# Two graph layers with gathers: the first gathers ahead of the flag, own rows multiplied in their own round, finish in four parts

## The chip, the cores and the metric

The kernel runs on one core of a Trainium2 chip. The metric is the time of one execution on the device in microseconds (us); the median of the runs is given with their lowest and highest. One more execution was profiled: its trace has each instruction of each engine, and the lines shown come from it. The engines are TensorE (PE; its weight loads are PEld), VectorE (DVE), ScalarE (ACT), GpSimd (POOL) and SyncE (SP, which only issues DMAs here).

## The reference

6250 nodes with 512 features; 106,250 edges `src`, `dst`, sorted by `dst` (100,000 random ones, each in both directions, and a loop for each node). Two layers, each an average over neighbours, two products and a normalization:

```python
# layer 0 (edges gathered by src, averaged at dst)
x_l = x @ W_l.T + b_l
agg = segment_sum(x_l[src], dst); deg = segment_sum(1, dst)
x = layernorm(x + agg / max(deg, 1) + x @ W_r.T)
# layer 1 (edges gathered by dst, averaged at src)
msg = h[dst] @ W_neigh.T + b_neigh
neigh = segment_sum(msg, src) / max(deg, 1)
out = relu(h @ W_self.T + b_self + neigh)
y = h + out
x = layernorm(x + layernorm(y) * gamma + beta)
```

All in float32. Since a product is linear, the kernel averages the rows first and multiplies the average.

## The kernel before

**Sorting.** `Sorter` holds the edges of a layer as tiles of 128: `node` (whose average an edge belongs to) and `idx` (which row it brings), both [128, 896]. For layer 0 the order is given: `as_given` (L333) loads keys, values and the keys shifted by one, turns them with TensorE and counts neighbours that are out of order (`mixed`, L373). A branch on `mixed` (L895) would sort; it isn't taken with these inputs. `place` (L450) finds the windows of nodes, writes their starts `lo`, the offsets `rel`, and a `flag` (L492), 0 when the grouped form fits. Layer 1 is sorted on DVE and TensorE; its steps are handed to layer 0's rounds as `other` (`more`, L768).

**Pools.** A pool keeps, for each tile name, as many buffers as its `bufs` says; `const` has one. `idx` is named `f"idx{layer}"` (L228).

**Rounds.** `grouped` (L585) works in Q rounds (60 in layer 0, 66 in layer 1). Round g takes four windows of up to 32 nodes, one for each quarter of the edges; the last rounds have three. Its edges lie in three or four tiles per window, and each tile of a window is one gather: an indirect DMA on GpSimd that brings 128 rows of 512 floats (`fetch`, L613; `gather`, L608). The rows go into `rows`, ten buffers of four gathers each. `match` (L627) makes 0/1 matrices on DVE, `shrink` their column sums; `visits` (L691) adds the rows into `agg` with TensorE, a tile at a time; `count` and `average` make `mean`. `begin` (L675) loads the window's own rows with SP; for layer 0's rounds 56 and 57 with a gather on GpSimd (L683). `turn` transposes `own` or `mean` through the one PSUM buffer `tp`, copied out by ACT (L576); `dense` multiplies it with w_r or w_l into `po` (one buffer in layer 0, two in layer 1). `close` runs the first part of the finish, `store` the second, and writes the rows with SP, or in the last rounds with GpSimd.

**Order.** The order on each engine is the order in which the instructions are written: the loop at L778. In round g: the gathers of g + 1, visits(g) to the first two tiles, turn(g - 1, mean), dense(g - 1, own), store(g - 2), begin(g + 1), visits to the third tile, dense(g - 1, mean), turn(g, own), the rest of visits(g), count, average, close(g - 1), then a piece of layer 1's sort. Each engine has its own queue, and an instruction that waits holds up what is behind it in that queue. Layer 1's gathers read `h_d`, which layer 0 writes, so they begin when its last row is stored.

Of the kernel before, what the change touches and what calls it, by code (L numbers as in the profile page):

```python
# [19 lines left out]
C = 4  # L20
# [78 lines left out]
def kernel(  # L99
# [109 lines left out]
    class Sorter:  # L209
# [123 lines left out]
        def as_given(self):  # L333


            full = M - 1
            ints, f32 = [], []
            for i, (v, fill, skip) in enumerate(((self.key, NONE, 0), (self.val, 0, 0),
                                                 (self.key, NONE, 1))):
                t = self.pool.tile([P, blocks, P], I32, name=("key_i", "val_i", "next_i")[i])  # L340
                nc.vector.memset(t[:, full // P:, :], fill)
                eng = nc.sync
# [12 lines left out]
                if i < 2:  # L355
                    f = self.pool.tile([P, blocks, P], F32, name="srt", bufs=2)
                    nc.vector.tensor_copy(f, t)
                    f32.append(f)
            for f, o in zip(f32, (self.node, self.idx)):
                p = self.ps.tile([P, 2 * D], F32, name="turn")  # L360
# [3 lines left out]
                nc.vector.tensor_copy(o[:, D:W], p[:, D:W])  # L364
            nxt = ints[2]
            nc.vector.tensor_tensor(nxt, ints[0], nxt, op=ALU.is_gt)
            worst = self.pool.tile([P, 1], F32, name="worst")
# [3 lines left out]
            nc.tensor.matmul(p[:1, :1], worst, ones[:, :1], start=True, stop=True)  # L371
            self.mixed = const.tile([1, 1], I32, name=f"mixed{self.layer}")
            nc.vector.tensor_copy(self.mixed, p[:1, :1])  # L373

# [75 lines left out]
        def place(self):  # L450
# [6 lines left out]
            nc.vector.memset(bad, 0.0)  # L457
            if self.loops:
                nc.vector.tensor_copy(bad[:, 2 * NW + C:], self.odd)
            ends = self.ps.tile([P, 2 * D], F32, name="turn")  # L460
# [67 lines left out]


    def finish0(nr, po, own, some, work):  # L530
        po = po[:nr]
        nc.vector.scalar_tensor_tensor(po, biases["bl"][:nr], some[:nr], po,
                                       op0=ALU.mult, op1=ALU.add)
        v = work.tile([P, D], F32, name="v", bufs=1)
        both(v[:nr], po, own[:nr], ALU.add)
        mv, root = spread(v[:nr], nr, work)
# [5 lines left out]
    def finish1(nr, po, own, some, work):  # L542
        po = po[:nr]
        if some is None:
            both(po, po, biases["bs + bn"][:nr], ALU.add)
        else:
            nc.vector.scalar_tensor_tensor(po, biases["bn"][:nr], some[:nr], po,
                                           op0=ALU.mult, op1=ALU.add)
            both(po, po, biases["bs"][:nr], ALU.add)
        nc.vector.scalar_tensor_tensor(po, po, 0.0, own[:nr], op0=ALU.max, op1=ALU.add)  # L550
        mv, root = spread(po, nr, work)
# [32 lines left out]

    def grouped(s, table, w_n, w_s, layer, finish, dest, other):  # L585


        with tc.tile_pool(name=f"g{layer}", bufs=2) as work, tc.tile_pool(
            name=f"gp{layer}", bufs=1, space=PSUM
        ) as ps:  # L590
            M, NW, Q = s.M, s.NW, s.Q
            chunks, hots, state = {}, {}, {}
            ends = Q - 1, (NW - 1) % Q, (NW - 2) % Q
# [13 lines left out]

            def gather(t, m):  # L608
                nc.gpsimd.indirect_dma_start(  # L609
                    out=t, out_offset=None, in_=table,  # L610
                    in_offset=bass.IndirectOffsetOnAxis(ap=s.idx[:, m:m + 1], axis=0))

            def fetch(g):  # L613
                for t in ([-1] if g == 0 else []) + list(own_tiles(g)):
                    rows = work.tile([P, C, D], F32, name="rows", bufs=CHUNKS)
                    chunks[t] = {}
                    for c in windows(g):
                        m = c * (Q // 2 * s.pair) + t
                        if 0 <= m < M:
                            gather(rows[:, c, :], m)  # L620
                            chunks[t][c] = rows[:, c, :]

# [120 lines left out]

            def close(g):
                st = state[g]
                st["finish"] = finish(st["nr"], st["po"], st["own"], st["some"], work)
                next(st["finish"])

# [26 lines left out]
            shrink(0)  # L775
            fetch(0)
            begin(0)
            for g in range(Q + 1):  # L778
# [116 lines left out]
    with tc.If(mixed > 0):  # L895
# [20 lines left out]

    f0 = nc.values_load(s0.flag[:1, :1], min_val=0, max_val=2 * s0.NW + C)
    with tc.If(f0 == 0) as cmp:
        grouped(s0, x, *w0, 0, finish0, h_d, sort_and_place(s1))
    with cmp.Else():  # L920
        drain(sort_and_place(s1))
        plain(s0, x, *w0, 0, finish0, h_d)

# [4 lines left out]
    with tc.If(f1 == 0) as cmp:  # L928
        grouped(s1, h_d, *w1, 1, finish1, out, iter(()))
    with cmp.Else():  # L930
# [29 lines left out]
```

## Time and profile before

| | us |
|---|---|
| median of 3 runs | 2129.82 (2129.74 to 2130.59) |
| the profiled execution | 2130.99 |
| its span, first to last instruction | 2129.2 |
| first gather of layer 0 | 30.38 |
| first gather of layer 1 | 1111.16 |
| last gather | 2095.39 |

The granted TensorE clock was 0.984 of full speed on average. A page line of a group gives: line, engine, operation, output<-inputs, number | busy us, mean ns of one | idle us just before them and what ended it. A line of the timeline gives: start, length, engine, line, operation, output<-inputs, shape, number [idle before <- what ended it]. A line of the chain gives: start, length, what the end of the run depended on then. `issue` is time without a wait that the profile shows.

### The profile page before, as it was taken

The page shows a single profiled execution, that of the slowest core. Times are in us where ns is not written, and L with a number is a line of the kernel's source. Part 1 is how long each engine was busy: PE and PEld are TensorE (multiplying, and loading weights), DVE is VectorE, ACT ScalarE, POOL GpSimd, SP SyncE. Part 2 cuts the span into 40 slices and gives each one's busy share as a digit, 9 for nine tenths or more (in the row PEclk, how much of TensorE's full clock was granted, in tenths as well). Part 3 has the DMA queues.
Part 4 walks back from the last instruction along what each step waited for, and adds up shares of the span by engine and source line. Part 5 has one row for each costly group of instructions (what it writes and reads, how often), then busy time and mean ns, then how long its engine had stood idle before and what let it go on. Part 6 is the DMA issues. An engine that isn't in the chain of part 4 may idle for free.

```text
span 2129.2 us, 26081 instructions
## 1 busy us (share of the span) xinstructions
PE 1945.1 (91%) x7723; PEld 671.4 (32%) x7723; DVE 1185.0 (56%) x2495; ACT 314.6 (15%) x661; POOL 1554.9 (73%) x1638
## 2 busy tenths in 40 slices
PE   4699999999999998999879999999999999999996
PEld 1132333332323333433222333333333333333332
DVE  2574455564555564342433666666666666666576
ACT  0011111111111111111111111111111111111111
POOL 3777777777777777777747777777777777777773
PEclk9899999999999999999989999999999999999998
DMA  7787877878887878888757888888888888888883
GB/s 225 224 242 235 238 237 237 240 238 240 238 239 237 239 236 240 246 237 242 223 151 227 243 246 246 245 246 244 246 242 249 240 249 241 247 242 246 241 247 109
DMA packets 184527, 499.36 MB, mean 235 GB/s; under 512 B 43946, under 2 KB 46436, under 8 KB 184366
## 3 DMA queue, kind: packets, MB, share of 16 engines
q0 software_dynamic: 130128, 426.11, 67.8%
q1 hardware_dynamic: 51406, 65.89, 9.7%
q10 hardware_dynamic: 2832, 5.51, 0.7%
q8 instruction: 66, 1.08, 0.2%
q14 instruction: 95, 0.78, 0.1%
HBM read 464.74 MB, written 32.96 MB: 234 GB/s over the span
## 4 chain that ended last, share of the span: by engine, by line
DMA 32%; POOL 28%; PE 22%; issue 14%; DVE 3%; POOLq 0%; ACT 0%; SPq 0%; DVEq 0%; ACTq 0%
POOL rows L609 28%; DMA rows<-h_d,idx 17%; DMA rows<-in_x_dram,idx 14%; PE po L582 10%; PE agg L700 9%; PE tp L574 2%; DMA val_i<-in_dst_dram 0%; DVE stats L514 0%; PE turn L465 0%; DVE po L173 0%; DMA own<-in_x_dram,slots 0%; PE deg L709 0%; PE turn L438 0%; PE turn L294 0%; DVE agg L727 0%
## 5 line engine op out<-in xcount | busy, mean ns | idle before, releaser
L700 PE MATMUL agg<-rows,hot 128*32 128x512 f32 x4220 | 900.3, 612 | 134.0 <-DMA rows<-in_x_dram,idx 46.1
L609 POOL DMA_INDIRECT rows<-in_x_dram,idx x834 | 800.7, 960 | 266.4 <-issue 224.7
L609 POOL DMA_INDIRECT rows<-h_d,idx x785 | 744.9, 949 | 242.6 <-issue 200.3
L582 PE MATMUL po<-wa,meanT 128*128 128x512 f32 (+1 forms) x1008 | 466.0, 605 | 0.0
L582 PE MATMUL po<-wb,ownT 128*128 128x512 f32 (+1 forms) x1008 | 456.3, 596 | 0.1
L700 PEld LDWEIGHTS agg<-rows,hot 128*32 128x32 f32 x4220 | 157.0, 109 | 655.0 <-DMA rows<-in_x_dram,idx 242.0
L565 DVE TENSOR_SCALAR inv<-deg 128x1 f32<-128x1 f32 (+1 forms) x60 | 9.5, 158 | 490.4 <-PE deg L709 490.4
L582 PEld LDWEIGHTS po<-wa,meanT 128*128 128x128 f32 (+1 forms) x1008 | 180.2, 188 | 286.7 <-issue 256.5
L582 PEld LDWEIGHTS po<-wb,ownT 128*128 128x128 f32 (+1 forms) x1008 | 181.8, 190 | 183.6 <-issue 183.4
L576 ACT COPY ownT<-tp 128x512 f32<-128x512 f32 (+1 forms) x126 | 73.3, 582 | 800.6 <-PE tp L574 800.6
L718 DVE TENSOR_SCALAR loops<-deg 128x1 f32<-128x1 f32 (+1 forms) x66 | 10.4, 158 | 310.9 <-PE deg L709 302.4
L173 DVE SCALAR_TENSOR_TENSOR srt<-srt 128x448 f32<-128x448 f32 (+3 forms) x313 | 180.4, 617 | 4.0
L731 ACT ACTIVATE mean<-agg,inv 128x512 f32<-128x512 f32 (+1 forms) x126 | 86.6, 687 | 359.3 <-DVE some L568 147.2
L640 DVE TENSOR_REDUCE hotb<-hot 128x128 bf16<-128x512 f32 (+1 forms) x126 | 133.8, 1062 | 0.1
L518 ACT ACTIVATE rstd<-mv,eps 128x1 f32<-128x1 f32 (+1 forms) x192 | 56.5, 294 | 438.9 <-DVE mv L516 435.6
L576 ACT COPY meanT<-tp 128x512 f32<-128x512 f32 (+1 forms) x126 | 73.1, 580 | 193.0 <-PE tp L574 192.9
L173 DVE SCALAR_TENSOR_TENSOR hot<-rel,cols 128x640 f32<-128x640 f32 x126 | 98.1, 778 | 0.2 <-DVE bs L173 0.2
L574 PEld LDWEIGHTS tp<-ident,mean 128*128 128x128 f32 (+1 forms) x504 | 52.8, 141 | 110.7 <-issue 43.5
L574 PE MATMUL tp<-ident,mean 128*128 128x128 f32 (+1 forms) x504 | 82.8, 287 | 4.8 <-ACT mean L731 4.8
L574 PEld LDWEIGHTS tp<-ident,own 128*128 128x128 f32 (+1 forms) x504 | 62.7, 141 | 72.8 <-issue 69.7
L574 PE MATMUL tp<-ident,own 128*128 128x128 f32 (+1 forms) x504 | 75.7, 273 | 5.4 <-DMA own<-in_x_dram,slots 5.4
L524 DVE TENSOR_SCALAR po<-po,mv,rstd 128x512 f32<-128x512 f32 (+1 forms) x66 | 54.0, 818 | 2.4
(151 smaller groups left out, 900.1 us busy)
## 6 DMA issues: line engine op xcount, KB each, us to landing
own<-h_d SPq DMA_DIRECT2D x261, 64.0 KB
out_dram<-y SPq DMA_DIRECT2D x250, 64.0 KB
own<-in_x_dram SPq DMA_DIRECT2D x230, 64.0 KB
h_d<-y SPq DMA_DIRECT2D x227, 64.0 KB
rows<-in_x_dram,idx POOLq DMA_INDIRECT x834
rows<-h_d,idx POOLq DMA_INDIRECT x785
wa<-in_L_gnn_W_l_dram ACTq DMA_DIRECT2D x1, 1024.0 KB
wb<-in_L_gnn_W_r_dram ACTq DMA_DIRECT2D x1, 1024.0 KB
```

Source lines behind the costliest of these rows:

```text
L173: nc.vector.scalar_tensor_tensor(o, a, 1.0, b, op0=ALU.mult, op1=op)
L518: nc.scalar.activation(root[:nr], mv[:nr, 1:2], AF.Sqrt, bias=eps[:nr])
L524: nc.vector.tensor_scalar(y, v, mv[:nr, 0:1], root[:nr], op0=ALU.subtract, op1=ALU.mult)
L565: nc.vector.tensor_scalar(inv[:nr], deg, 1.0, None, op0=ALU.max)
L574: nc.tensor.transpose(p[:, k, :nr], v[:nr, k * P:(k + 1) * P], ident[:nr, :nr])
L576: nc.scalar.copy(t[:, :, :nr], p[:, :, :nr])
L582: nc.tensor.matmul(po[:nr], aT[:, k, :nr], w[:, k, :], start=first and k == 0, stop=end and k == NK - 1)
L609: nc.gpsimd.indirect_dma_start(out=t, out_offset=None, in_=table, in_offset=bass.IndirectOffsetOnAxis(ap=s.idx[:, m:m + 1], axis=0))
L640: nc.vector.tensor_reduce(hb[:, 0, :], hots[g][:, s.X * C:n * C].rearrange("p (v c) h -> p (c h) v", c=C), axis=mybir.AxisListType.X, op=A ...
L700: nc.tensor.matmul(agg[H * c:H * (c + 1), :], hot[:, C * (s.X + v) + c, :], chunks[t][c], start=t == ts[0], stop=t == ts[-1])
L718: nc.vector.tensor_scalar(st["loops"][:nr], deg[:nr, 1:2], 1.0, None, op0=ALU.add)
L731: nc.scalar.mul(st["mean"][:nr], st["agg"][:nr], st["inv"][:nr])
```

## The change

Layer 0's first gathers (19, for tiles -1 to 3) are issued ahead of everything that depends on keys: their indices come by four small loads on ACT's queue straight from the list of values (`first_rows`), into a tile of `const` named `idx0`. The `mixed` branch is gone; its number goes into the flag, and the sort stands in the flag's other branch. In `as_given` the shifted keys are loaded by ACT, keys are turned first, and the values' turn comes back as a function that runs after `place`. The `rows` buffers lie in a pool of their own that both layers use. In the loop dense(g, own) is now in round g, after average(g); in the last round it stands ahead of the last visits. turn(g, own) stands ahead of dense(g - 1, mean). The finish runs in four parts: `ready`, two `follow`, `store`. finish0 adds bias and own rows before the product; finish1 adds own rows and beta at the start and then needs two operations for normalizing, gamma, beta and own rows.

```diff
@@ as_given
-            for i, (v, fill, skip) in enumerate(((self.key, NONE, 0), (self.val, 0, 0),
-                                                 (self.key, NONE, 1))):
+            for i, (v, fill, skip, eng) in enumerate((
+                (self.key, NONE, 0, nc.sync), (self.key, NONE, 1, nc.scalar),
+                (self.val, 0, 0, nc.sync),
+            )):
...
+            def columns(t, o):
+                f = self.pool.tile([P, blocks, P], F32, name="srt", bufs=2)
+                nc.vector.tensor_copy(f, t)
                 p = self.ps.tile([P, 2 * D], F32, name="turn")
                 for b in range(blocks):
                     nc.tensor.transpose(p[:, b * P:(b + 1) * P], f[:, b, :], ident)
                 nc.scalar.copy(o[:, :D], p[:, :D])
                 nc.vector.tensor_copy(o[:, D:W], p[:, D:W])
+            columns(key, self.node)
...
-            self.mixed = const.tile([1, 1], I32, name=f"mixed{self.layer}")
-            nc.vector.tensor_copy(self.mixed, p[:1, :1])
+            odd = self.pool.tile([1, 2], F32, name="mixed")
...
+            return lambda: columns(val, self.idx)
+
+        def first_rows(self):
+            n = 1 + self.half
+            self.idx0 = const.tile([P, C, n], I32, name="idx0")
+            for c in range(C):
+                a = c * (self.Q // 2 * self.pair) - 1
+                k = max(0, -a)
+                v = self.val[(a + k) * P:(a + n) * P]
+                nc.scalar.dma_start(self.idx0[:, c, k:], v.rearrange("(t p) -> p t", p=P))
@@ place
-            if self.loops:
-                nc.vector.tensor_copy(bad[:, 2 * NW + C:], self.odd)
+            nc.vector.tensor_copy(bad[:, 2 * NW + C:], self.odd)
@@ finish0
-        po = po[:nr]
-        nc.vector.scalar_tensor_tensor(po, biases["bl"][:nr], some[:nr], po,
+        v = work.tile([P, D], F32, name="v")
+        nc.vector.scalar_tensor_tensor(v[:nr], biases["bl"][:nr], some[:nr], own[:nr],
                                        op0=ALU.mult, op1=ALU.add)
-        v = work.tile([P, D], F32, name="v", bufs=1)
-        both(v[:nr], po, own[:nr], ALU.add)
+        yield
+        both(v[:nr], po[:nr], v[:nr], ALU.add)
+        yield
@@ finish1
+        add = work.tile([P, D], F32, name="add")
+        both(add[:nr], own[:nr], biases["be"][:nr], ALU.add)
+        yield
...
-        normalize(po, po, mv, root, nr)
-        both(po, po, biases["ga"][:nr], ALU.mult)
-        both(po, po, biases["be"][:nr], ALU.add)
+        nc.vector.reciprocal(root[:nr], root[:nr])
+        nc.vector.scalar_tensor_tensor(po, po, mv[:nr, 0:1], biases["ga"][:nr],
+                                       op0=ALU.subtract, op1=ALU.mult)
         y = work.tile([P, D], F32, name="y")
-        both(y[:nr], po, own[:nr], ALU.add)
+        nc.vector.scalar_tensor_tensor(y[:nr], po, root[:nr], add[:nr],
+                                       op0=ALU.mult, op1=ALU.add)
@@ the loop of rounds
             if g < Q:
                 visits(g, slice(0, 2))
-            if g:
-                turn(g - 1, "mean")
-                dense(g - 1, "own")
             if g > 1:
                 store(g - 2)
             if g + 1 < Q:
                 begin(g + 1)
+            end = g == Q - 1
+            if g:
+                turn(g - 1, "mean")
+            if g < Q and not end:
+                visits(g, slice(2, 3))
             if g < Q:
-                visits(g, slice(2, 3))
+                turn(g, "own")
             if g:
                 dense(g - 1, "mean")
+                follow(g - 1)
+            if end:
+                visits(g, slice(2, 3))
+                dense(g, "own")
             if g < Q:
-                turn(g, "own")
                 visits(g, slice(3, None))
                 count(g)
                 average(g)
             if g:
-                close(g - 1)
+                follow(g - 1)
+            if g < Q:
+                if not end:
+                    dense(g, "own")
+                ready(g)
@@ the order of the whole
+    rpool = ctx.enter_context(tc.tile_pool(name="rows", bufs=1))
...
-    s0.as_given()
+    s0.first_rows()
+    first = {t: gathered(s0, x, t, range(C), s0.idx0) for t in range(-1, s0.half)}
+    rest = s0.as_given()
     biases["bl"] = row_bcast(b_l, "bl_t")
     w0 = load_weights(w_l, w_r, 0)
-    mixed = nc.values_load(s0.mixed[:1, :1], min_val=0, max_val=P)
-    with tc.If(mixed > 0):
-        make_signs(spool)
-        drain(s0.runs())
     s0.place()
+    rest()
```

`gathered` issues one tile's gathers for the given windows, as `fetch` did, into `rows` of the new pool; with `idx0` it takes the indices from the small tile.

More of the change, by code (lines that the diff above doesn't have):

```diff
@@ L336, in as_given @@
             full = M - 1
-            ints, f32 = [], []
-            for i, (v, fill, skip) in enumerate(((self.key, NONE, 0), (self.val, 0, 0),
-                                                 (self.key, NONE, 1))):
-                t = self.pool.tile([P, blocks, P], I32, name=("key_i", "val_i", "next_i")[i])
+            ints = []
+            for i, (v, fill, skip, eng) in enumerate((
+                (self.key, NONE, 0, nc.sync), (self.key, NONE, 1, nc.scalar),
+                (self.val, 0, 0, nc.sync),
+            )):
+                t = self.pool.tile([P, blocks, P], I32, name=("key_i", "next_i", "val_i")[i])
                 nc.vector.memset(t[:, full // P:, :], fill)
-                eng = nc.sync
                 a = full // P
@@ L354, in as_given @@
                 ints.append(t)
[L355 to L359, printed above, removed]
+            key, nxt, val = ints
+            def columns(t, o):
+                f = self.pool.tile([P, blocks, P], F32, name="srt", bufs=2)
+                nc.vector.tensor_copy(f, t)
                 p = self.ps.tile([P, 2 * D], F32, name="turn")
@@ L364, in as_given @@
                 nc.vector.tensor_copy(o[:, D:W], p[:, D:W])
-            nxt = ints[2]
-            nc.vector.tensor_tensor(nxt, ints[0], nxt, op=ALU.is_gt)
+            columns(key, self.node)
+            nc.vector.tensor_tensor(nxt, key, nxt, op=ALU.is_gt)
             worst = self.pool.tile([P, 1], F32, name="worst")
@@ L371, in as_given @@
             nc.tensor.matmul(p[:1, :1], worst, ones[:, :1], start=True, stop=True)
-            self.mixed = const.tile([1, 1], I32, name=f"mixed{self.layer}")
-            nc.vector.tensor_copy(self.mixed, p[:1, :1])
+            odd = self.pool.tile([1, 2], F32, name="mixed")
+            nc.vector.memset(odd, 0.0)
+            nc.vector.tensor_copy(odd[:, :1], p[:1, :1])
+            self.odd = odd
+            return lambda: columns(val, self.idx)
[7 more added lines that the diff above has]
+                nc.scalar.dma_start(self.idx0[:, c, k:], v.rearrange("(t p) -> p t", p=P))
         def unpack(self):
@@ L550, in finish1 @@
         nc.vector.scalar_tensor_tensor(po, po, 0.0, own[:nr], op0=ALU.max, op1=ALU.add)
+        yield
         mv, root = spread(po, nr, work)
         yield
-        normalize(po, po, mv, root, nr)
-        both(po, po, biases["ga"][:nr], ALU.mult)
-        both(po, po, biases["be"][:nr], ALU.add)
+        nc.vector.reciprocal(root[:nr], root[:nr])
+        nc.vector.scalar_tensor_tensor(po, po, mv[:nr, 0:1], biases["ga"][:nr],
+                                       op0=ALU.subtract, op1=ALU.mult)
         y = work.tile([P, D], F32, name="y")
-        both(y[:nr], po, own[:nr], ALU.add)
+        nc.vector.scalar_tensor_tensor(y[:nr], po, root[:nr], add[:nr],
+                                       op0=ALU.mult, op1=ALU.add)
         mv, root = spread(y[:nr], nr, work)
@@ L583, in project, with gathered, grouped @@
                              start=first and k == 0, stop=end and k == NK - 1)
-    def grouped(s, table, w_n, w_s, layer, finish, dest, other):
+    def gathered(s, table, t, windows, idx):
+        rows = rpool.tile([P, C, D], F32, name="rows", bufs=CHUNKS)
+        got = {}
+        for c in windows:
+            m = c * (s.Q // 2 * s.pair) + t
+            if 0 <= m < s.M:
+                at = idx[:, m:m + 1] if idx is s.idx else idx[:, c, t + 1:t + 2]
+                nc.gpsimd.indirect_dma_start(
+                    out=rows[:, c, :], out_offset=None, in_=table,
+                    in_offset=bass.IndirectOffsetOnAxis(ap=at, axis=0))
+                got[c] = rows[:, c, :]
+        return got
+    def grouped(s, table, w_n, w_s, layer, finish, dest, other, chunks):
         with tc.tile_pool(name=f"g{layer}", bufs=2) as work, tc.tile_pool(
@@ L591, in grouped @@
             M, NW, Q = s.M, s.NW, s.Q
-            chunks, hots, state = {}, {}, {}
+            hots, state = {}, {}
             ends = Q - 1, (NW - 1) % Q, (NW - 2) % Q
@@ L606, in own_tiles @@
                              g // 2 * s.pair + (s.pair if g % 2 else s.half))
[L608 to L611, printed above, removed]
             def fetch(g):
                 for t in ([-1] if g == 0 else []) + list(own_tiles(g)):
[L615 to L621, printed above, removed]
+                    chunks[t] = gathered(s, table, t, windows(g), s.idx)
             def visit_tiles(g):
@@ L742, in dense, with ready, follow @@
                         v == "own", v == "mean")
-            def close(g):
+            def ready(g):
                 st = state[g]
                 st["finish"] = finish(st["nr"], st["po"], st["own"], st["some"], work)
+                next(st["finish"])
+            def follow(g):
+                st = state[g]
                 next(st["finish"])
@@ L775, in grouped @@
             shrink(0)
-            fetch(0)
+            if not chunks:
+                fetch(0)
             begin(0)
@@ L914, in sort_and_place @@
         yield True, s.place
-    f0 = nc.values_load(s0.flag[:1, :1], min_val=0, max_val=2 * s0.NW + C)
+    f0 = nc.values_load(s0.flag[:1, :1], min_val=0, max_val=2 * s0.NW + C + 2)
     with tc.If(f0 == 0) as cmp:
-        grouped(s0, x, *w0, 0, finish0, h_d, sort_and_place(s1))
+        grouped(s0, x, *w0, 0, finish0, h_d, sort_and_place(s1), first)
     with cmp.Else():
         drain(sort_and_place(s1))
+        drain(s0.runs())
         plain(s0, x, *w0, 0, finish0, h_d)
@@ L928 @@
     with tc.If(f1 == 0) as cmp:
-        grouped(s1, h_d, *w1, 1, finish1, out, iter(()))
+        grouped(s1, h_d, *w1, 1, finish1, out, iter(()), {})
     with cmp.Else():
```

## The prediction

> **What bounds it now.** I read the page first (engines, groups), then GpSimd's rows in order of time, then both layers' ends in the timeline and the chain. The page:
>
> ```profile
> span 2129.2 us, 26081 instructions
> PE 1945.1 (91%) x7723; PEld 671.4 (32%) x7723; DVE 1185.0 (56%) x2495; ACT 314.6 (15%) x661; POOL 1554.9 (73%) x1638
> ...
> L609 POOL DMA_INDIRECT rows<-in_x_dram,idx x834 | 800.7, 960 | 266.4 <-issue 224.7
> L609 POOL DMA_INDIRECT rows<-h_d,idx x785 | 744.9, 949 | 242.6 <-issue 200.3
> ```
>
> TensorE looks fuller (91%), but its busy time is stretched where it waits for rows; GpSimd is the pacemaker. One gather is 0.95 us plus 0.30 of issue: its rows start every 1.252 us for a thousand microseconds. 834 + 2 own gathers in layer 0 make 1047 us, 785 in layer 1 make 983. The rest of the span: 30 before the first gather, 24 between the layers' gathers (1087.6 to 1111.2), 33 after the last (2096.3), 12 lost between gathers. The timeline of the start and of layer 0's end, and the chain's pieces (start, length) there:
>
> ```profile
> 16.44 0.15 DVE L373 CAST mixed<-turn 1x1 int32<-1x1 f32 x1 [0.37 <-PE turn L371]
> 23.08 0.06 DVE L455 MEMSET node<- 128x1 f32 x1 [6.50 <-DVEq L895]
> 28.84 0.14 DVE L492 CAST flag<-nbad 1x1 int32<-1x1 f32 x1
> 30.38 1.13 POOL L609 DMA_INDIRECT rows<-in_x_dram,idx  x1 [12.70 <-issue]
> 54.36 0.95 POOL L609 DMA_INDIRECT rows<-in_x_dram,idx  x1 [0.30 <-issue]
> ...
> 1046.67 3.60 DMA own<-in_x_dram,slots
> 1050.41 1.09 PE tp L574 x4
> 1079.18 3.57 DMA rows<-in_x_dram,idx
> 1095.69 7.12 PE po L582 x16
> 1106.62 0.93 POOL L753 DMA_INDIRECT h_d<-y,slots  x1 [13.82 <-DVE y L524]
> 1111.16 1.00 POOL L609 DMA_INDIRECT rows<-h_d,idx  x1 [3.61 <-DVE hot L173]
> ```
>
> A gather cannot start before the flag; the mixed branch alone holds DVE 6.5 us. 54.36 is the 20th gather, the first of round 1. At the end the owner is TensorE: it stands still until 1050.3 for the own rows of round 56, then works through with one wait for rows (about 1.2 us, to 1082.75).
>
> **Part 1, the first gathers moved ahead of the flag.** When does the 20th gather start?
>
> - First index load, S. ACT issues four small loads from 0.76; one issue is about 0.45 (key_i's took 0.48). The first gather has no window 0, so it waits for the second: issued by 1.7, and a small load here lands some 1.95 after its issue began (last key piece 4.21, its cast 6.16). Each load is 512 or 640 pieces of 4 bytes. The Trainium skill, "DMA: Bandwidth & Descriptors", Rules for kernel authors, speaks against them: a last dimension that isn't contiguous becomes one descriptor per element. The nearest row is the 128-byte stores of the tail in the DMA view of 30 to 34 us:
>
> ```profile
> q1 hardware_dynamic: 901, 0.12, 18.3%
> ```
>
> 18.3% of 16 engines in 4 us over 901 packets is 13 ns each, so 40 per engine cost 0.5 us a load, not the price of a bulk load. S = 4.3; ends 3.3 (nothing shared with key_i) and 7.0 (60 ns each, two loads in a row).
> - Nineteen gathers: 53.10 - 30.38 = 22.7 to the start of the 19th.
> - They now lie beside DVE's casts. The Trainium skill, "SBUF — State Buffer", Who interferes with whom: a DVE operation in a two-port mode and GpSimd exclude each other for the whole instruction. The trace has it, two gathers beside one sign flip:
>
> ```profile
> 136.87 1.18 POOL L609 DMA_INDIRECT rows<-in_x_dram,idx  x1 [0.30 <-PE agg L700]
> 137.26 0.39 DVE L331 TENSOR_SCALAR srt<-srt 128x448 f32<-128x448 f32 x1
> 138.36 1.31 POOL L609 DMA_INDIRECT rows<-in_x_dram,idx  x1 [0.30 <-issue]
> ```
>
> They lose 0.23 + 0.36 to an operation of 0.39. By the rule two casts of 0.63 (L357) cost 1.3, scaled from the row 1.9; not all of a cast meets a gather: 1.0, ends 0 and 1.9.
> - A new wait. The small index tile has the same name as layer 0's index tile ("idx0"), in a pool with one buffer per name: the built program gives both one address, and both copies into the large one (ACT, then DVE) wait for all nineteen gathers to have landed; the next gather waits for ACT's. A gather lands 3.6 after its start (1046.67 to 1050.27); beside other loads up to 5.3 (31.81 to 37.06). I take 3.7: w_l and w_r, issued near 10, should be through by 25. Then ACT's copy 0.59 and two handshakes, 0.85.
>
> Sum: 4.3 + 22.7 + 1.0 + 3.7 + 0.85 = 32.6 against 54.4: **-21.8** (ends 30.4 and 37.8: -24.0, -16.6). What hides behind it: the key columns, comparison and placing follow as before, without the branch, so the flag comes near 20, the val transposes near 25, and GpSimd's flag read and branch (1.4, from 28.98 to 30.38) fit beside the landing. If key landed 7 us later, that cover is gone and every further microsecond counts. Behind ACT's waiting copy are six issues for layer 1's weights and biases (needed 1000 us later) and ACT's branch; ownT is wanted near 38. Behind DVE's copy are tail, branch and hot(0): TensorE starts near 34.5 instead of 34.1 and SP's tail store and own loads near 33, as before, but with all rows of round 0 there. Its slack takes this up: ten row tiles are 50 us of gathers. The 3 MB of layer 1's loads now run beside gathers, which stretches landings but no pace, since eight may be under way (10 us).
>
> **Part 2, own product in its own round.** Per round nothing is added: eight passes of 3.53, moved. While gathers set the pace it is free; a round needs 12.2 to 12.4 of TensorE (count to count, 2079.58, 2091.78, 2104.19) against 15.03 of twelve gathers. New waits inside: turn(own) for ACT's meanT copy (0.59, behind one tile of 1.0), dense(own) for DVE's read of po in layer 0 (0.69, behind the last tiles). DVE now waits in mid-round for dense(mean); behind it are count and the sort steps, due 12 us later, and DVE has 9 us of work there.
>
> At layer 0's end it costs. Own rows of rounds 56 and 57 come by gathers queued behind their round's rows. Today TensorE has finished dense(55, mean) when it stands; afterwards turn(56, own) is ahead of it, so at 1050.4 these 3.5 us are still to do. Both orders then have the same products left. Added: 3.5, 0.8 for turn(59, own) behind a copy with nothing between, 0.7 for the last meanT copy, no longer under dense(own). Taken off: the 1.2 wait for rows at 1082.75, 0.75 for the bias operation (L532, now early), 0.3 as the cold clock after the standstill costs some 2.3 on today's visits (1051.4 to 1055.0 for what takes 2.0) and would cost 2.0 on the product. **+2.7** (ends 0, if it catches up, and +5.5, if the cold clock of 1050 to 1054 lasts over the product). The jump to layer 1 is unchanged; its first gather waits on five fewer events of 0.05: -0.2.
>
> **Part 3, layer 1's end**, in timeline rows:
>
> ```profile
> 2104.19 0.25 PE L709 MATMUL deg<-ones_b,hotb 128*96 128x1 bf16 x2
> 2106.55 0.90 PE L574 MATMUL tp<-ident,mean 96*128 96x96 f32 x4 [2.12 <-ACT mean L731]
> 2107.25 4.97 PE L582 MATMUL po<-wb,ownT 128*96 128x512 f32 x8
> 2112.05 3.60 PE L582 MATMUL po<-wa,meanT 128*96 128x512 f32 x8
> 2115.68 0.69 DVE L173 SCALAR_TENSOR_TENSOR po<-po,bs 96x512 f32<-96x512 f32 x1 [2.11 <-PE po L582]
> ```
>
> No wait for rows is left here: TensorE is behind since round 62, so the last own product only moves ahead of the count: 2104.2 becomes 2107.7, turn(mean) begins 2.4 later as now, takes 0.5, meanT's copy, now bare, 0.6, and dense(mean), between the warm 3.60 and the cold 4.97, 4.3. It ends at 2115.5, today at 2115.6: -0.1. The finish gets shorter: 0.81 + 3 x 0.69 (normalize, gamma, beta, own) become two of 0.7, with gaps 7.95 becomes 6.4: **-1.5** (ends -3 and +1). The fewer DVE operations elsewhere lie under gathers: nothing.
>
> **Sum**: -21.8 + 2.7 - 0.2 - 1.6 = -20.9. The profiled execution took 2130.99 (span 2129.2, 1.8 around it), 1.2 above the median 2129.82; I apply the difference to the median: 2108.9.
>
> **Rivals.**
> A. As above, 2108.9 (its own range 2104 to 2115). Chance 0.70.
> B. The index loads are slow (100 ns a piece: two loads 8 us, S near 11) and everything after follows: 15 gained at the start, 2116. For: no row has 4-byte pieces. Against: the 13 ns. 0.11.
> C. The own product fills standstill at both ends after all (the chain gives TensorE 22% of the span): 3.5 off each end, instead of +2.7 and -0.1: 2099. For: dense(own) is in today's last chain at both ends. Against: only one wait for rows in the last 50 us. 0.12.
> D. **Slower**: TensorE becomes the bound in layer 1's rounds. Place: turn(mean), ACT's copy, turn(own), dense(mean) now run in series on one transpose buffer. The round would have to grow from 12.4 beyond 15.03; each 0.1 above costs 66 x 0.1 = 6.6, and the gain is gone at 15.35. Two bare copies with handshakes add 1.6 (14.0); at 15.6 the time is 2109 + 38 = 2147. 0.06. Nothing in the rows gives the missing 1.3.
> The first gathers not coming earlier at all can't be: no flag stands ahead of them. 0.01 for what I don't see.
>
> **Numbers.** The range reaches over B and C: 2101 to 2117. About 0.2% (4 us) is what a measurement here tells from no change. Faster 0.93 (A, B, C), same 0.01, slower 0.06.
>
> **What would show it.** First gather at 3.3 to 7; a hole of 3 to 5 us in GpSimd's rows before the 20th, ended by ACT's idx copy, the 20th near 32.6; then 1.252 without holes; TensorE standing until own of round 56 lands, longer than today's 5.4; layer 0's last h_d store about 19 after the shift, not 22; the finish after the last product about 6.4. Wrong: a first gather past 8, holes in GpSimd's rows in mid-layer (D), or layer 0's tail shorter than now (C).

## The result, and the profile after

| | us |
|---|---|
| before, median | 2129.81 (2129.74 to 2130.59) |
| after, median | 2165.5 (2162.78 to 2172.06) |
| ratio | 1.0169, 95% interval 1.0156 to 1.0182 |
| predicted | 2108.9 (2101 to 2117), faster |

The change makes the kernel 1.7% slower; the forecast had the wrong sign. (In two groups of runs below, e5 to e8 and e9 to e12, TensorE was granted 0.86 to 0.89 of its clock in the mean and the kernel before takes 2530 and 2534 us; their ratios stand against that, and "less clock" below means these runs.)

The page of the changed kernel, its span, engines, and the two groups of gathers:

```profile
span 2161.0 us, 26124 instructions
PE 1977.0 (91%) x7723; PEld 659.9 (31%) x7723; DVE 1127.5 (52%) x2431; ACT 310.2 (14%) x661; POOL 1574.0 (73%) x1638
...
L614 POOL DMA_INDIRECT rows<-in_x_dram,idx x834 | 808.3, 969 | 290.7 <-issue 206.8
L614 POOL DMA_INDIRECT rows<-h_d,idx x785 | 756.3, 963 | 241.7 <-issue 199.3
```

A gather takes 969 and 963 ns in the mean, where it took 960 and 949. The timeline of the start:

```profile
5.71 1.13 POOL L614 DMA_INDIRECT rows<-in_x_dram,idx  x1 [4.00 <-DMA idx<-in_src_dram]
33.07 0.59 ACT L364 CAST idx<-turn 128x512 int32<-128x512 f32 x1 [22.02 <-DMA rows<-in_x_dram,idx]
33.92 0.96 POOL L614 DMA_INDIRECT rows<-in_x_dram,idx  x1 [3.90 <-ACT idx L364]
34.31 0.66 SPq L940 DMA_DIRECT2D h_d<-tail  x1
36.67 23.58 SPq L713 DMA_DIRECT2D own<-in_x_dram  x8
60.12 1.09 PE L595 MATMUL tp<-ident,own 128*128 128x128 f32 x4 [19.25 <-DMA own<-in_x_dram]
70.97 1.00 POOL L614 DMA_INDIRECT rows<-in_x_dram,idx  x1 [12.12 <-PE agg L725]
81.20 1.09 DVE L258 TENSOR_TENSOR next_i<-key_i,val_i 128x896 int32<-128x896 int32 x1 [6.40 <-DMA val_i<-in_dst_dram]
91.16 6.12 PE L603 MATMUL po<-wb,ownT 128*128 128x512 f32 x8 [13.86 <-DVE inv L586]
98.57 1.39 POOL L614 DMA_INDIRECT rows<-in_x_dram,idx  x1 [17.88 <-PE agg L725]
```

The 20th gather is at 33.9, 20 us sooner than before. Then GpSimd stands twice (a "hole" below is such a stand between two gathers), 12.1 and 17.9 us, with all ten row tiles full, because TensorE stands: first for the own rows of round 0, then for VectorE, which is in the sort's first loads. Counted out in GpSimd's rows, for both kernels and for those experiments that ran where before takes 2130 (start of the named gather or store in us, ratio of times with its 95% interval; e14 also has a shorter finish for the last block):

| | 20th gather | 60th | last of layer 0 | first of layer 1 | last | last store | ratio |
|---|---|---|---|---|---|---|---|
| before | 54.4 | 106.4 | 1086.7 | 1111.2 | 2095.4 | 2123.9 | |
| after | 33.9 | 114.5 | 1102.8 | 1129.0 | 2124.5 | 2155.7 | 1.0169 |
| e1 weights early | 36.3 | 100.7 | 1086.8 | 1114.3 | 2118.0 | 2149.1 | 1.0121 (1.0104 to 1.0137) |
| e2 own name | 30.1 | 106.5 | 1092.3 | 1120.0 | 2121.7 | 2152.0 | 1.0153 (1.0136 to 1.0170) |
| e3 parts 2 and 3 | 54.7 | 107.1 | 1092.8 | 1120.5 | 2119.3 | 2151.1 | 1.0118 (1.0101 to 1.0135) |
| e4 part 1 | 34.5 | 106.6 | 1086.5 | 1110.3 | 2093.6 | 2120.0 | 0.9994 (0.9986 to 1.0003) |
| e13 part 2 | 54.8 | 107.3 | 1087.5 | 1116.2 | 2099.4 | 2139.9 | 1.0080 (1.0064 to 1.0097) |
| e14 part 1 mended | 30.4 | 80.7 | 1067.2 | 1091.0 | 2075.8 | 2102.1 | 0.9914 (0.9898 to 0.9931) |
| e15 parts 1, 2 mended | 30.5 | 80.6 | 1074.5 | 1102.8 | 2086.8 | 2123.1 | 0.9997 (0.9990 to 1.0003) |
| e16 the same, store behind | 30.4 | 80.4 | 1073.4 | 1101.8 | 2085.8 | 2113.5 | 0.9965 (0.9957 to 0.9972) |

The differences between the first two rows, column by column, account for the 31.8 between the two profiled spans (the medians differ by 35.7; the profiled execution of after is its fastest): -20.4 to the 20th gather, +28.5 to the 60th (the two holes), +8.0 to layer 0's last, +1.7 to layer 1's first, +11.3 to the last, +2.6 to the last store.

### The profile page after: what moved, and what is told of

Its sections match the earlier page's. It is cut to its first block, busy times and chain, and to the rows that moved or that the text cites. A ratio compares the mean times of both kernels' runs of the same rounds, so it can differ in the third digit from the quotient of the medians.

```text
span 2161.0 us, 26124 instructions
## 1 busy us (share of the span) xinstructions
PE 1977.0 (91%) x7723; PEld 659.9 (31%) x7723; DVE 1127.5 (52%) x2431; ACT 310.2 (14%) x661; POOL 1574.0 (73%) x1638
## 4 chain that ended last, share of the span: by engine, by line
PE 30%; DMA 27%; POOL 25%; issue 12%; DVE 3%; SPq 0%; ACT 0%; POOLq 0%; DVEq 0%; ACTq 0%
POOL rows L614 25%; PE po L603 15%; DMA rows<-in_x_dram,idx 14%; PE agg L725 11%; DMA rows<-h_d,idx 11%; PE tp L595 2%; DMA h_d<-tail 1%; DVE stats L528 0%; PE deg L734 0%; DVE hotb L665 0%; DMA own<-h_d 0%; DMA val_i<-in_dst_dram 0%; PE turn L294 0%; SPq L789 0%; DVE y L577 0%
## 5 line engine op out<-in xcount | busy, mean ns | idle before, releaser
L725 PE MATMUL agg<-rows,hot 128*32 128x512 f32 x4220 | 921.2, 606 | 98.3 <-DMA rows<-in_x_dram,idx 51.7
L614 POOL DMA_INDIRECT rows<-h_d,idx x785 | 756.3, 963 | 241.7 <-issue 199.3
L603 PE MATMUL po<-wb,ownT 128*128 128x512 f32 (+1 forms) x1008 | 466.3, 605 | 14.2 <-DVE inv L586 14.2
L603 PE MATMUL po<-wa,meanT 128*128 128x512 f32 (+1 forms) x1008 | 458.4, 598 | 3.8 <-ACT meanT L597 3.8
L173 DVE SCALAR_TENSOR_TENSOR po<-po,bs 128x512 f32<-128x512 f32 (+1 forms) x66 | 46.1, 699 | 346.4 <-PE po L603 346.4
L173 DVE SCALAR_TENSOR_TENSOR v<-po,v 128x512 f32<-128x512 f32 (+1 forms) x60 | 41.3, 689 | 254.2 <-PE po L603 254.2
L595 PE MATMUL tp<-ident,own 128*128 128x128 f32 (+1 forms) x504 | 82.9, 288 | 32.6 <-DMA own<-in_x_dram 19.3
L595 PEld LDWEIGHTS tp<-ident,own 128*128 128x128 f32 (+1 forms) x504 | 53.1, 142 | 138.1 <-issue 123.8
```

What stands on the lines that cost most here:

```text
L173: nc.vector.scalar_tensor_tensor(o, a, 1.0, b, op0=ALU.mult, op1=op)
L595: nc.tensor.transpose(p[:, k, :nr], v[:nr, k * P:(k + 1) * P], ident[:nr, :nr])
L603: nc.tensor.matmul(po[:nr], aT[:, k, :nr], w[:, k, :], start=first and k == 0, stop=end and k == NK - 1)
L614: nc.gpsimd.indirect_dma_start(out=rows[:, c, :], out_offset=None, in_=table, in_offset=bass.IndirectOffsetOnAxis(ap=at, axis=0))
L725: nc.tensor.matmul(agg[H * c:H * (c + 1), :], hot[:, C * (s.X + v) + c, :], chunks[t][c], start=t == ts[0], stop=t == ts[-1])
```

## The experiments

Four theories were tried. **T1**: the tail store (zeros into the last rows of `h_d`, 2048 pieces) lies beside 3 MB of layer 1's weights and holds the own loads, hence the first hole. **T2**: the second hole is VectorE's stand in the sort's loads, with GpSimd too far ahead. **T4**: operations of the new finish hold gathers back. **T5**: at layer 1's end a square root stands ahead of meanT's copy on ScalarE. (The expectations also name T3, that own rows are late for another reason than the tail; e1 ruled it out.)

**The first hole.** The DMA queues of the changed kernel from 40 to 48 us (q1 is SP's, q10 ScalarE's: packets, MB, share of 16 engines), then those of before around its tail store, 32 to 36 us:

```profile
q0 software_dynamic: 578, 1.90, 59.7%
q10 hardware_dynamic: 622, 1.16, 38.9%
q1 hardware_dynamic: 622, 0.08, 6.3%
```

```profile
q0 software_dynamic: 147, 0.51, 47.6%
q1 hardware_dynamic: 2064, 0.26, 44.9%
```

Before, the tail passed at 2064 packets in 4 us. Now its 128-byte packets take turns with the weights' packets of some 1.9 KB: 622 against 622, and in the order of their starts the two counts never differ by more than 3. From 50 to 54 us, with 34 packets left on ScalarE's queue, SP's passes 1053. The Trainium skill, "DMA: Bandwidth & Descriptors", Queues, rings and completion order, has each DMA engine take turns between the queues by packets; that fits. It calls 9 to 17 descriptors a typical packet; the records of the tail hold one piece of 128 bytes each, and they alternate singly. The chain of the changed kernel (start, length, what the end depended on), and the longest wait of SP's queue among the own loads:

```profile
34.31 21.57 DMA h_d<-tail
...
56.70 3.17 DMA own<-in_x_dram
59.87 0.25 issue
60.12 1.09 PE tp L595 x4
...
SPq L713 <- DMA h_d<-tail: 5.6, 1, 5.6
```

SP's issue of the first own load took 12.3 (36.67 to 48.97), and the third, at 55.89, was issued only when the tail had landed.

e1, the weights' loads alone moved:

```diff
+    w1 = load_weights(w_neigh, w_self, 1)   # and the four row_bcasts: moved up, from behind the tail
     s0.place()
     rest()
```

> The changed kernel with one edit: layer 1's weight and bias loads are issued ahead of the placing and the val columns, not behind ScalarE's late copy into idx. Theory T1 (the tail store takes turns with 3 MB of weights and holds the own loads, and the second hole only follows from the lead lost in the first): the tail store is through in about 5 us instead of 21.6, own rows of round 0 land near 41 instead of 60, no hole over 2 us in GpSimd's rows between 34 and 110, the 60th gather near 86 instead of 114.5; time 2137 (2133 to 2143), still above the kernel before, since the gathers' longer cadence and the ends stay. Rival T2 (the second hole has a cause of its own, VectorE's wait for the sort's loads with a lead that ten row tiles can't carry): the first hole of 11.8 goes, one of 10 or more near 80 stays; 2148 to 2154. Rival T3 (own rows are late for another reason than the tail): no change, 2165.

Own rows came at 47.98 and the first hole went; a hole of 13.4 at 72 stayed. The 60th gather came 13.8 sooner, the time fell only by 0.5% since this run's gathers in layer 1 took 974 ns. T2 as rival was right, T1 alone was not enough.

e2, the name alone: `name="idx0"` becomes `name="firsts"`.

> The changed kernel with one edit: the small index tile gets a name of its own, so the copies into the large one no longer wait for nineteen gathers. Weights and tail are still issued within a microsecond of each other. T1: the copy is at 25 instead of 33, the 20th gather at 30 to 31 instead of 33.9, the tail still takes about 20 us beside the weights but ends near 47, own rows land near 52; both holes stay with the first a little shorter; everything behind moves about 8 earlier: 2157 (2153 to 2162). Rival (the shared name is all of the loss): the holes go, 2137. Rival T3 (tail and weights are not the cause): only the 3 of the 20th gather, 2162.

The copy came at 25, the tail at 25.85, and the eight own issues still took 25.1 us beside the weights; the holes were 8.8 and 17.9. The shared name costs 8 us up to the 60th gather; of these 3.6 remained at the last store, since the mean gather of layer 1 was longer in this run (971 ns; with this finish it is 963 to 974). It isn't the main loss.

**Parts alone.** e3 takes the start of before with the loop and finish of after, e4 the reverse.

> The kernel before with the second and third part of the change alone: own product in its own round, finish in four parts; the start (branch, sort of the loads, first gathers) as before. Theory T4 (the finish's new operations that touch SBUF alone, add and v, hold back each gather that starts inside them, 8 in layer 0 and 11 in layer 1, and the ends cost 1.7 and 2.6): 2130 + 23 = 2153 (2148 to 2160), mean gather 0.963 in layer 1. Rival (the longer cadence belongs to the earlier start or to the place of the operations, not to parts 2 and 3): 2130 to 2136.

> The kernel before with the first part of the change alone: gathers ahead of the branch; loop and finish as before. T1 and T4: the 20th gather near 34, the first hole of about 12 as in the changed kernel, since the own turn stood ahead of the last visits of round 0 before too; the second shorter by the own product (6), about 11; then the cadence of before: 2130 - 20.4 + 11.8 + 11.5 = 2133 (2127 to 2140). Rival (the order of the own product makes the holes): no hole, 2109 to 2113.

e3 measured +1.2%, as T4 said: the loss without the new start is in the gathers and the ends. e4 measured no change: two holes eat the whole gain of the start, also with the old order.

```profile
65.56 0.94 POOL L608 DMA_INDIRECT rows<-in_x_dram,idx  x1 [6.15 <-PE agg L719]
91.28 0.94 POOL L608 DMA_INDIRECT rows<-in_x_dram,idx  x1 [15.91 <-PE agg L719]
```

**The gathers' cadence.** A row of GpSimd and two of VectorE in the changed kernel's timeline:

```profile
1337.22 0.66 DVE L173 SCALAR_TENSOR_TENSOR add<-own,be 128x512 f32<-128x512 f32 x1
1337.25 1.45 POOL L614 DMA_INDIRECT rows<-h_d,idx  x1 [0.30 <-issue]
1337.79 1.03 DVE L665 TENSOR_REDUCE hotb<-hot 128x128 bf16<-128x512 f32 x1
```

The gather begins inside `add`, whose two inputs lie in SBUF, the memory of most tiles (the products lie in PSUM), and takes 1.45 instead of 0.946. e5 puts the arithmetic of before into the new order, with the start of before:

```diff
     def finish1(nr, po, own, some, work):
-        add = work.tile([P, D], F32, name="add")
-        both(add[:nr], own[:nr], biases["be"][:nr], ALU.add)
         yield
...                                  # finish0 likewise
+        normalize(po, po, mv, root, nr)
+        both(po, po, biases["ga"][:nr], ALU.mult)
+        both(po, po, biases["be"][:nr], ALU.add)
+        both(y[:nr], po, own[:nr], ALU.add)
```

> The kernel before with the second part of the change alone: own product in its own round and the finish cut into its parts, but with the finish's arithmetic of before (all its operands in or through PSUM, no add, no SBUF-only v). T4 (SBUF-only operations of the finish hold the gathers back): the mean gather of layer 1 is back at 0.949 from 0.968 and that of layer 0 at 0.960 from 0.967; the ends' 3.2 and 3.3 stay, one of the finish's 1.6 comes back on top: 2131 + 8 = 2139 (2135 to 2142). Rival (the place of VectorE's operations in the round sets the cadence): mean gather stays at 0.965 or more, 2155.

It ran with less clock: ratio 1.0448 (1.0426 to 1.0470). Holes of 2.5 us and more (two over 5.7: 7.0 and 8.3) lie in nearly every round of layer 1, nearly all ended by TensorE: there TensorE sets the pace. How long it stood ahead of the transposes of own rows is the first number behind the second bar (e5, then e13, the same kernel with more clock):

```profile
L579 PE MATMUL tp<-ident,own 128*128 128x128 f32 (+1 forms) x504 | 115.4, 371 | 418.6 <-ACT meanT L581 169.1
```

```profile
L579 PE MATMUL tp<-ident,own 128*128 128x128 f32 (+1 forms) x504 | 82.5, 287 | 18.0 <-DMA own<-in_x_dram,slots 9.4
```

In two rounds of e5, from 1608 to 1640 us, meanT's copy comes right behind a square root on ScalarE (1617.36 and 1617.56, 1634.88 and 1635.08), and TensorE waits 4.9 and 3.6: with less clock what T5 says of layer 1's end happens inside the layer too. Why the kernel before takes 2530 there isn't shown. e9 is the same kernel.

> The same kernel as in the run with the order alone, which met a chip that gave TensorE less clock (before took 2530 there, so TensorE and not GpSimd set the pace). On a chip where before takes 2130: T4 as said there, mean gather 0.949 in layer 1 and 0.960 in layer 0, 2139 (2135 to 2142). Rival (the place of VectorE's operations in the round): mean gather 0.965 and more, 2155. On a slow chip again: a ratio near 1.045, as TensorE's round is then the longer one and the new order makes it longer.

1.0398 (1.0371 to 1.0426), with less clock again. e12, the changed kernel with the old finish1 alone, met the same:

> The changed kernel with one edit: layer 1's finish has the arithmetic of before, in four parts; layer 0 is as changed and serves as control. T4: mean gather of layer 1 0.949 to 0.952 instead of 0.963, of layer 0 unchanged at 0.967 to 0.970; ratio to before falls by 0.004 to 0.005 from 1.0169 (-11 in the gathers, +1.6 at the end): 2156 where before takes 2130. Rival (the order): layer 1's mean gather stays at 0.963.

1.0215 (1.0171 to 1.0259). Its 946 ns in layer 1 decides nothing: e8, with the new arithmetic, has 947 with less clock too, probably since gathers that wait for tiles begin at other moments. e13 is the kernel of e5 a third time.

> The order alone once more (own product in its own round, arithmetic of before), since the two runs of it met chips with less TensorE clock. Where before takes 2130: T4 (the SBUF-only operations of the finish made the longer cadence): mean gather of layer 1 at 0.949, of layer 0 at 0.960, 2139 (2135 to 2142). Rival (the place of VectorE's operations in the round): 0.965 and more, 2155. Where before takes over 2500: ratio 1.04 as before.

Layer 1's gathers on the page of e3 and of e13, which differ in the finish's arithmetic alone:

```profile
L600 POOL DMA_INDIRECT rows<-h_d,idx x785 | 759.6, 968 | 241.7 <-issue 199.3
```

```profile
L598 POOL DMA_INDIRECT rows<-h_d,idx x785 | 743.9, 948 | 242.1 <-issue 205.4
```

T4 holds for the cadence: from first to last gather the new arithmetic costs 5.3 in layer 0 and 15.6 in layer 1. The time, 2148, is between the two forecasts, since layer 1's end came out 12 longer than before, not 3.3 + 1.6.

**The second hole.** e6 is e4 with `if g >= 6:` ahead of both `more(...)`, so that the sort begins six rounds later.

> The kernel with the early start alone and one more edit: layer 1's sort begins in round 6 instead of round 0. T2 (the second hole is VectorE standing in the sort's first loads while GpSimd is twenty gathers ahead, which ten row tiles can't carry; six rounds later TensorE has used the lead up): the hole of 15.9 at 75 goes, the one of 6.2 at 59 stays, no new hole at round 6; 2129 - 16 = 2113 (2111 to 2118). Rival (TensorE can't keep the lead in any case, the tiles are full for its own pace): holes of the same sum come elsewhere, 2126 to 2130.

Ratio 0.984 (0.9822 to 0.9857), with less clock. The hole near 80 went (none over 3.6 between 69 and 190), that of 9.0 at 59 stayed, as T2 has it. But here many holes of 2 to 3.6 follow, ended by TensorE, so that the rival isn't excluded by this run; e14 excludes it.

e7 adds e1's and e2's edits, e10 also the short finish for the last block alone (a `finish_last`, its `add` done behind the average).

> The early start alone with its three troubles taken away: the small index tile has its own name, layer 1's weights are issued ahead of the placing, the sort begins in round 6. Loop and finish as before. T1, T2: the 20th gather near 30.2, own rows of round 0 long landed, no hole over 2 us between 31 and 1040; 2131 - 24 = 2107 (2104 to 2111). Rival (3 MB of weights beside the first gathers slow these): the 20th gather at 33 to 36, 2111 to 2114.

> The early start with its three troubles taken away (own name for the small index tile, layer 1's weights ahead of the placing, sort from round 6), loop and finish as before, and the short finish for layer 1's last block alone, its add done ahead. T1, T2 where before takes 2130: 20th gather at 30 to 31, no hole over 2 between 31 and 1040, the last finish 6.6 instead of 8.2: 2131 - 24 - 1.6 = 2105 (2102 to 2110). Rival (TensorE is late for another reason, and the ten row tiles run full): a hole of 6 to 9 before 66, 2112 to 2116. On a slow chip: ratio 0.984 as before.

0.9842 (0.9816 to 0.9867) and 0.980 (0.9769 to 0.9832), with less clock; against what was expected, a hole (8.7 and 8.5) at 55 remained, and in e10 own rows were turned at 56.9: the weights, though issued early, were still under way when the tail began at 30.9 (from 36 to 40 us 379 packets of each queue, again one for one). e11 mends the changed kernel with all this:

> The changed kernel with its whole order (own product in its own round, four parts) and everything mended that the runs have named: own name for the small index tile, weights ahead of the placing, sort from round 6, the finish's arithmetic of before, at the very end the transpose of the mean ahead of the store. If these are all that cost (T1, T2, T4, T5): 2105 + 1.6 and what the order costs at the ends, 3 in layer 0 and 0.5 in layer 1: 2110 (2106 to 2115), mean gather 0.949 in layer 1. Rival (the own product's place costs more in itself): 2120 and up.

1.0305 (1.0271 to 1.0338), with less clock, so that its 2110 was not tested. e14 takes the order of before, as e10, and moves whatever isn't wanted at the start:

```diff
+    def layer_loads(): ...           # layer 1's two weights and four bias rows, as before
+    def end_rows(): ...              # the tail store, as before
     def sort_and_place(s):
+        yield False, layer_loads
+        yield False, end_rows
         yield False, lambda: make_signs(spool)
...
+                if g >= 6:
                     more(1, True)
```

> The early start with everything that isn't wanted at the start moved to round 6: the tail store, layer 1's weights and biases, the sort; own name for the small index tile; short finish for the last block. T1 and T2: the 20th gather near 30.5, own rows of round 0 land by 38 (57 with tail and weights still beside them), TensorE never over 5 without rows to 110, no hole over 2 in GpSimd's rows on a chip where before takes 2130: 2131 - 24 - 1.6 = 2105 (2102 to 2110). Rival (the 20 early gathers can't be turned into time, since TensorE starts no earlier): a hole of 6 or more before 110, 2115 and up. Where before takes over 2500: ratio 0.975 to 0.98.

2112.2 where before takes 2132.5: the early gathers do become time, and this version beats both kernels by 0.9% and more (2.2 of its 20 us come behind the last gather, where it has the short finish). Its start in the timeline, and its largest hole in layer 0:

```profile
30.35 0.96 POOL L624 DMA_INDIRECT rows<-in_x_dram,idx  x1 [0.16 <-issue]
33.40 0.66 PE L605 MATMUL tp<-ident,own 128*128 128x128 f32 x4
...
176.12 0.94 POOL L624 DMA_INDIRECT rows<-in_x_dram,idx  x1 [3.65 <-PE agg L735]
```

The 24 us at the 20th gather are 19.5 at layer 0's last: this hole, and gathers of up to 1.64 beside the sort's first operations. e15 has this start with the changed order and the old finish throughout:

> The changed kernel's order with the same start as the run beside it (all that isn't wanted moved to round 6), the arithmetic of before, and the last mean's transpose ahead of the store. Where before takes 2130: 3.5 to 5 above the run beside it (3 at layer 0's end, 0.5 at layer 1's, 1.6 for the last finish): 2110 (2106 to 2114). Rival (own product's place costs in every round): 2120 and up. Where before takes over 2500 (TensorE sets the pace): about 1.03 to 1.04.

2131.7: my 2110 fell. Of the 19.5 above e14, 1.6 is e14's short finish; the order costs the rest, some 18. Three places, against e14: a hole of 13.0 instead of 3.7 where the sort begins (in layer 0 the own product waits for VectorE to read the one `po`, at 176.26 to 176.95, and VectorE is in the sort until 174), which leaves 7.4 at layer 0's last gather; 4.4 more between the layers; 10.0 more after the last gather, with the 1.6.

**Layer 1's end.** e8 is the changed kernel with one edit:

```diff
+                if g == Q:
+                    turn(g - 1, "mean")      # was behind the store
                 if g > 1:
                     store(g - 2)
```

> The changed kernel with one edit in its last step alone: the transpose of the last mean and its copy stand ahead of the store of the last but one block, as before, not behind it. Theory T5 (at layer 1's end the meanT copy waits on ScalarE behind the square root of that block's second normalisation, and TensorE for the copy, 3.2 us, and then runs cold): the copy starts some 2.4 sooner, last product ends 3 sooner, 2165.5 - 3 = 2162 on the first chip; from count to the first operation of the finish 9 instead of 12.0. Rival (TensorE's cold clock alone makes the end): less than 1.

1.0199 (1.0176 to 1.0221), with less clock, where the changed kernel itself was not run. The rows decide; after, then e8:

```profile
2142.46 0.29 ACT L532 ACTIVATE rstd<-mv,eps 96x1 f32<-96x1 f32 x1 [2.73 <-DVE mv L530]
2142.66 0.46 ACT L597 COPY meanT<-tp 128x384 f32<-128x384 f32 x1
2143.17 5.81 PE L603 MATMUL po<-wa,meanT 128*96 128x512 f32 x8 [3.20 <-ACT meanT L597]
```

```profile
2560.56 0.48 ACT L597 COPY meanT<-tp 128x384 f32<-128x384 f32 x1 [0.33 <-PE tp L595]
2561.09 3.67 PE L603 MATMUL po<-wa,meanT 128*96 128x512 f32 x8 [0.62 <-ACT meanT L597]
2562.96 0.29 ACT L532 ACTIVATE rstd<-mv,eps 96x1 f32<-96x1 f32 x1 [1.92 <-DVE mv L530]
```

From the count (the `deg` product, 2137.06 in the changed kernel) to the finish's first operation it took 7.3 instead of 12.0; the clock granted during the product was 0.62 in the changed kernel (2143 to 2149) and 1.00 in e8 (2561 to 2565). e16 does the same in every round, on e15:

> The changed order with everything mended, as in the run before it, and one more edit: the store of the last but one block (whose second normalisation puts a square root into ScalarE's queue) stands behind the transpose of the mean in every round, not in the last alone. T5 (at layer 1's end TensorE waits in each round for a meanT copy that stands behind that square root, 3 x 2.1): these three waits go, from the last gather to the last store 30 instead of 36.3; 2131.7 - 6 = 2126 (2122 to 2129) where before takes 2132, and layer 0's end no longer than now. Rival (the waits are taken over by the next link, VectorE's chain to the mean): under 2 gained, 2130 and more. Where before takes over 2500: no ratio told, the waits in the last rounds are read all the same.

2124.5, 7.2 less; from the last gather to the last store 27.8 instead of 36.3. The waits of TensorE for ScalarE from 2040 on (us in total, times, longest) in e15 and in e16:

```profile
PE tp L593 <- ACT meanT L595: 6.0, 3, 2.1
PE tp L593 <- ACT mean L754: 2.1, 1, 2.1
PE po L601 <- ACT meanT L595: 0.6, 1, 0.6
```

```profile
PE tp L593 <- ACT mean L754: 2.1, 1, 2.1
```

T5 holds: with 27.8, e16's end is within 0.1 of e14's 26.3 plus the 1.6 of the short finish. With the old finish its price is higher (e13's end is 40.5, 12 above before; there TensorE waits 4.7 for the last copy, not 3.2); the new finish hid part of it.

## Why the prediction was wrong, point by point

- **The start** was right: first gather 5.71 (said 4.3, ends 3.3 and 7), a hole of 4.1 ended by ScalarE's idx copy (said 3 to 5), 20th gather 33.9 (said 32.6), -20.4 instead of -21.8.
- **"Its slack takes this up: ten row tiles are 50 us of gathers"** failed, for 28.5. The tail store was where the step put it (34.3); its length beside the weights, 21.6 instead of some 4, and with it "stretches landings but no pace", was not asked: SP's own loads queue behind it. And a stand of TensorE of 19.8 us, for VectorE in the sort's first loads, was in the trace of before:

```profile
92.97 3.47 PE L700 MATMUL agg<-rows,hot 128*32 128x512 f32 x16 [19.82 <-DVE hot L173]
```

  There no gather waited for it; with gathers 20 us further ahead it reaches GpSimd. Of the row tiles' 50 us, some 20 were spent by being early. e1 and e14 show both, e6 the second; e4 shows that this alone takes the whole gain.
- **"The fewer DVE operations elsewhere lie under gathers: nothing"** failed, for 19.3 (8.0 and 11.3). Fewer, but two of the new ones, `add` and finish0's first, have both inputs in SBUF, where before the change all of the finish's arithmetic but the last normalization read PSUM. The Trainium skill, "SBUF — State Buffer", Who interferes with whom, says of an operation with two SBUF inputs that it contends with a GpSimd instruction that reads SBUF. The trace agrees (18 of 18, last section). The prediction took that section for the two casts only, and misread the rows that it showed for it. These two rows of before belong beside them:

```profile
136.08 1.15 DVE L173 SCALAR_TENSOR_TENSOR srt<-srt 128x448 f32<-128x448 f32 x2
137.69 3.55 DVE L173 SCALAR_TENSOR_TENSOR srt<-srt 128x448 f32<-128x448 f32 x6
```

  The gathers at 136.87 and 138.36 began inside these steps of the sort, which have two SBUF inputs; the sign flip began when the first was under way and had ended 0.7 before the second. The first had 0.36 of its step left and lost 0.23. So what the prediction put down to the sign flip was the cost that it then set at nothing. e3 against e13 shows it: 5.3 and 15.6.
- **Own product free in mid-layer** held for the pace at full clock (e13's layer 1 takes 983.2 from its first gather to its last, before 984.2). It fails where something stands: the hole where the sort begins is 9 longer (e15 against e14).
- **Layer 0's end**, said +2.7 (0 to 5.5): +1.7, in e13 +4.2. One term of its sum doesn't come out of its rows: visits of 3.6 for what takes 2.0 lose 1.6, not 2.3, and with 1.6 the sum is +3.4.
- **Layer 1's end**: the finish was right, 6.64 instead of 8.24, -1.6. The products were said -0.1 and measured +4.2 (2.6 + 1.6): "meanT's copy, now bare, 0.6" was 3.2 of wait and then a product of 5.81 at a granted clock of 0.62 (said 4.3), because the store, which the change moves ahead of turn(mean), puts a square root ahead of that copy on ScalarE. The step costed the moved product and not the moved store. Without that, e8 has 7.3 from the count to the finish's first operation, where the step reckoned 7.8 (2107.7 to 2115.5); e16 shows the same.
- **Rival D** had the sign, not the mechanism: in layer 1 no gather waits for TensorE here. With less clock it is what happens (e5, e9).

Between the profiled executions the forecast of -20.9 is off by 52.6: 1.4 at the start, 28.5 in the holes, 19.3 in the gathers, 4.2 at layer 1's end, and 0.8 less than said between the layers.

## What to carry to other kernels

What starts sooner runs into whatever was hidden while it was late: ask for each transfer that now lies beside another what it shares turns with, and for each stand of the next engine how much of the buffers the head start has already spent. An operation moved off PSUM, or a new one with both inputs in SBUF, is counted against GpSimd's gathers even when the sum of VectorE's work falls. When a step is moved, follow each engine's queue for all its instructions, the small ones too.

## What was not expected of the hardware

Packets of SP's and ScalarE's queues alternated one for one, whatever their size (622 of 128 bytes against 622 of some 1.9 KB), so the store of small pieces ran at the pace of the large ones.

The hold on a gather depends on where it begins. In layer 1 of the changed kernel (1180 to 2080 us) 18 gathers began inside an `add` and 22 inside the last normalization (SBUF to SBUF) with 0.2 or more of it left, and all 40 were held, for what was left of the operation less 0.13; of 241 that began inside other VectorE operations (with a PSUM operand, statistics, reductions) none was. 41 `add` that began with a gather or while one was already under way held nothing; 35 of them took their usual 0.66, six that began within 0.04 of the gather's start up to 0.72. So an `add` costs about 0.11 in the mean (6.7 us over 59), and the sum depends on how rounds and gathers happen to lie: 963 to 974 ns over four kernels. The last normalization, unchanged, holds 22 gathers for 5.1 us where before the change it held 10 for 1.4; why it is met more often wasn't tried, so that of layer 1's 11.3 some 3.7 have an open cause. In layer 0 (200 to 1040 us) finish0's first operation held 19 gathers for 6.0; in the kernel before, the sort's steps with two SBUF inputs held 32 there, for 5.8.
